# A graph-attention kernel: x loaded without zeros, first rows of Q made earlier, counting in steps, last norms side by side

## The chip, the core and the metric

The kernel runs on one core of a Trainium2 chip. A core has a matrix engine (PE; PEld is its weight load, which overlaps), a vector engine (DVE), a scalar engine (ACT), a general engine (POOL) that here issues the indirect gathers, and a queue engine (SP) that issues plain DMAs in program order. The metric is the device time of one execution in microseconds (us). All engines run their own instruction lists in order and wait for one another through semaphores.

## The reference

One layer of graph attention over 6250 nodes, 206250 edges sorted by destination, 128 features in 8 heads of 16, then a residual and a layer norm:

```python
Qh = (h @ WQ).reshape(N, H, D); Kh = (h @ WK).reshape(N, H, D); Vh = (h @ WV).reshape(N, H, D)
Eh = (edge_attr @ WE).reshape(-1, H, D)
score = jnp.einsum('ehd,ehd,ehd->eh', Kh[src], Qh[dst], Eh) * inv_sqrt_d
score = jnp.exp(jnp.clip(score, -5.0, 5.0))
msg = Vh[src] * score[:, :, None]
wV = jax.ops.segment_sum(msg, dst, num_segments=N)
Z = jax.ops.segment_sum(score, dst, num_segments=N)
h_out = wV / (Z[:, :, None] + 1e-06)
x = _layernorm(x + h_out.reshape(N, H * D), axis=-1)
```

So K and V are taken by source node (any node), Q by destination (sorted), E is a product per edge, and the sums run over edges with one destination.

## The kernel before, in words

Edges are cut into 1612 tiles of 128; four tiles make a batch, 406 batches in all (the last ones smaller). The work has a head, a loop over batches, and an end.

The head. x by features is loaded once into `xT_sb`, one column per node with a zero between every two columns (lines 113 to 116: twelve loads of an array of 2 x 6250 + 2 columns that the host has filled with zeros). The zeros belong to a trick in the loop: some tiles' columns of x are gathered on chip, two at a time, by OR-ing eight bytes (`columns`, line 371), and a zero neighbour leaves the other column as it is. The table `kv` (K and V of all nodes, in HBM) is made by `table` (line 255) in 13 groups of four blocks of 128 nodes: two engines copy from PSUM into one of two buffers `kvst`, and SP stores the buffer. Meanwhile POOL gathers rows of x for the first twelve batches (`gather`, line 392), whose K and V are then made on chip (`project`, line 412), so that they do not need the table. After the table come, in program order, `from_window(0)` (line 182), `build_q` (line 297), and the first loads `load_rel(0)` and `load_q` (lines 560 to 562).

`from_window(i)` takes the destinations of 128 (then 74) groups of eight tiles, subtracts the first node of the group, stores the result as `relD` in HBM, and counts how many edges lie within a window of 42 rows (`count`, line 175, three passes of DVE over 1024 columns). The counts prove at the end that the edges were sorted as assumed; if not, a slow path runs. `load_rel` reads `relD` back, spread over 126 partitions (`relb`). `q_rows` makes a block of 128 rows of Q as three bf16 parts, stored as `qs`; `load_q` reads the 126 rows that eight tiles need (`qw`).

The loop. For batch b, `stage_a` makes E (`eps`) and the expanded Q (`qps`) on PE; `stage_b`, one batch later, multiplies K with Q (`kq`, line 463), with E (`kqe`, 466), reduces (469) and clips (472) on DVE; `weigh` takes the exponential on ACT; `messages`, two batches later, multiplies V (`msg`, 507); `stage_c` adds up by destination on PE (`agg`, 529). Gathered rows lie in twelve buffers: POOL may gather batch b only when `msg` of batch b-12 is done. From batch 12 on gathers read `kv`. Three of every seven batches have one tile whose columns ACT and DVE copy on chip instead (lines 371 and 374). Between the stages `fill` (line 564) places one small DVE step at a time: of a block of Q, or of a layer norm.

From batch 12 on the order on each engine is the program's; before it a scheduler sets the order by readiness. SP issues its DMAs strictly one after another, and at most eight plain DMAs are in flight, as each reuses a semaphore.

The end. `finish` (line 495) shifts the sums of two blocks into place on PE, and `layernorm` (line 719) is a generator of small DVE steps. The last block is the lone one (`final`, line 522): when its last sum is made, all norms still open are run to their end first, and then its own.

Of the kernel before, what the change touches and what calls it, by code (L numbers as in the profile page):

```python
# [8 lines left out]
F32 = mybir.dt.float32  # L9
# [90 lines left out]
def edge_attention(ctx: ExitStack, tc: tile.TileContext, x, xT, srcT, srcC, dstT, dstB, dst0, bnd, lo, eaT,  # L100
# [12 lines left out]
    NX = 12  # L113
    cuts = [(2 * N + 2) * i // NX for i in range(NX + 1)]
    for a, b in zip(cuts, cuts[1:]):
        nc.sync.dma_start(spread[:, a:b], xT[:, a:b])
# [23 lines left out]
    with ExitStack() as fast:  # L140
# [34 lines left out]
        def count(rows, cl, vals, hi):  # L175

            nc.vector.tensor_scalar(cl, vals, 0.0, float(hi), op0=ALU.max, op1=ALU.min)
            nc.vector.tensor_tensor(cl, cl, vals, op=ALU.is_equal)
            nc.vector.tensor_reduce(cn[:rows, len(counts):len(counts) + 1], cl, axis=AX.X, op=ALU.add)
            counts.append(rows)  # L180

        def from_window(i):
# [7 lines left out]
            nc.vector.tensor_tensor(w[:k], d[:k, :1], bnd_c[:k, i:i + 1], op=ALU.min)  # L190
            r = ip.tile([P, WT * P], BF16, name="relq", bufs=1)
            nc.vector.tensor_scalar(r[:k], d[:k], w[:k], None, op0=ALU.subtract)
            nc.sync.dma_start(relD[a:a + k], r[:k])
            cl = wp.tile([P, WT * P], F32, name="clq", tag="kvst", bufs=2)
            count(k, cl[:k], r[:k], QW - 1)
# [25 lines left out]
        def count_inside():  # L221

            W = 4 * 2 * D
            for a in range(0, NT, W):
                e = min(NT, a + W)
                cl = wp.tile([P, W], F32, name="cl", tag="kvst", bufs=2)[:, :e - a]
                count(P, cl, rel[:, a:e], HW - 1)
# [26 lines left out]

        def table(b0):
            st = wp.tile([P, KB, 2 * D], F32, name="kvst", bufs=2)
            blocks = range(b0, min(NB, b0 + KB))
            for b in blocks:
                n = min(P, N - b * P)
                ps = pair_bank(b, "kvacc", [P, 2 * D])  # L260
                made = nc.tensor.matmul(ps[:n], xT_sb[:, b * P:b * P + n], wkv_sb,
# [3 lines left out]
                else:  # L265
                    nc.scalar.copy(st[:n, b - b0, :], ps[:n])
            full = [b for b in blocks if (b + 1) * P <= N]
# [244 lines left out]
        def stage_c(b):  # L512
            n, g, oh, m = st8.pop(b)
            for i in range(n):
# [39 lines left out]
        from_window(0)  # L554
        build_q(q_built(QLOOK + 2), True)
# [4 lines left out]
        load_rel(0)  # L560
        for j in range(QLOOK):
            load_q(j)
# [234 lines left out]
```

## Time and profile before

| | us |
|---|---|
| median of 3 runs | 1867.37 (1865.28 to 1867.83) |
| profiled execution | 1864.63 |
| its span, first to last instruction | 1862.8 |
| DVE busy | 1679.4 (90%) |
| ACT busy | 1623.1 (87%) |
| POOL busy | 1379.9 (74%) |
| PE busy | 1331.3 (71%) |
| gathers of rows of `kv` | 1401, 952 ns each |

How to read it. Times are of one execution, from the span's start. A line of the timeline has start, duration, engine, source line, operation, what is written and read, how many instructions were merged, and in brackets how long the engine was idle before and what it waited for. An engine's name with a q (SPq) is its instruction queue: issuing a DMA takes no busy time. A line of the table by stage has a stretch, its length, the busy time and number of instructions of each engine, the granted share of PE's clock, the share of time that the DMA engines were busy, and the rate they reached.

### The profile page before, as it was taken

How to read it: one execution, taken by the hardware profiler on the slowest of the kernel's cores; microseconds unless marked ns; L12 is line 12 of the kernel's file. 1: busy time of each engine (PE TensorE's matmuls, PEld its weight loads, DVE VectorE, ACT ScalarE, POOL GpSimd, SP SyncE). 2: the span in 40 equal slices, each digit the busy share in tenths (PEclk: the TensorE clock that was granted, in tenths of full speed). 3: DMA queues.
4: the chain of work that ended last, by engine and by line, in shares of the span. 5: the costliest groups of instructions: out<-in, count | busy, mean ns of one | idle time of the engine just before them, and what ended most of it. 6: DMA issues, size and time to landing. Idle time of an engine off the chain costs nothing.

```text
span 1862.8 us, 48831 instructions
## 1 busy us (share of the span) xinstructions
PE 1331.3 (71%) x9376; PEld 1163.7 (62%) x9376; DVE 1679.4 (90%) x6911; ACT 1623.1 (87%) x15506; POOL 1379.9 (74%) x1456
## 2 busy tenths in 40 slices
PE   4787777677776777676777776777767767677676
PEld 3576666666675666565666665666656656666665
DVE  3479999999999999999999999998999899998997
ACT  1236999899999999999999999999899999998993
POOL 6577777777777777777777777777777777777774
PEclk8898999899989998999999999898899899888998
DMA  9767757767777587677667667667766676667662
GB/s 316 220 196 213 219 179 209 207 201 207 207 215 208 180 241 199 184 217 228 192 209 228 190 191 225 203 185 214 219 203 186 195 231 191 195 192 227 207 195 70
DMA packets 171087, 381.63 MB, mean 205 GB/s; under 512 B 58478, under 2 KB 84412, under 8 KB 170774
## 3 DMA queue, kind: packets, MB, share of 16 engines
q0 software_dynamic: 68768, 186.80, 34.2%
q1 hardware_dynamic: 100866, 190.58, 33.7%
q14 instruction: 237, 1.94, 0.3%
q8 instruction: 76, 1.25, 0.3%
q10 hardware_dynamic: 1140, 1.06, 0.2%
HBM read 363.50 MB, written 14.81 MB: 203 GB/s over the span
## 4 chain that ended last, share of the span: by engine, by line
DVE 49%; PE 15%; DMA 12%; issue 6%; DVEq 6%; POOL 3%; ACT 0%; POOLq 0%
DMA kvrows<-kv,src 12%; DVE kqe L466 9%; DVE kq L463 9%; DVE xcol L371 8%; PE eps L453 6%; DVE sc L469 6%; DVE msg L507 5%; DVEq L364 5%; DVE onehot L431 5%; DVE onehotT L441 4%; PE agg L529 4%; POOL kvrows L401 3%; PE finps L492 3%; DVE sc L472 2%; PE qps L456 1%
## 5 line engine op out<-in xcount | busy, mean ns | idle before, releaser
L401 POOL DMA_INDIRECT kvrows<-kv,src x1401 | 1333.3, 952 | 441.9 <-issue 315.5
L374 ACT COPY xcol<-xT_sb 128x4 uint8 x14344 | 1442.7, 191 | 39.9 <-issue 33.9
L453 PE MATMUL eps<-we_sb,ea 128*128 128x128 f32 x3224 | 493.0, 300 | 446.5 <-issue 224.1
L453 PEld LDWEIGHTS eps<-we_sb,ea 128*128 128x128 f32 x3224 | 429.9, 206 | 538.6 <-issue 449.1
L529 PE MATMUL agg<-msg,onehot 128*128 128x136 f32 x3224 | 536.3, 314 | 34.0 <-DVE msg L507 23.2
L529 PEld LDWEIGHTS agg<-msg,onehot 128*128 128x128 f32 x3224 | 457.0, 212 | 86.1 <-DVE msg L507 83.5
L371 DVE TENSOR_TENSOR xcol<-xT_sb 128x8 uint8 x3260 | 301.8, 160 | 24.8 <-issue 22.2
L463 DVE TENSOR_TENSOR kq<-kvrows,qps 128x512 f32<-128x512 f32 x406 | 274.5, 676 | 51.0 <-DMA kvrows<-kv,src 26.7
L507 DVE TENSOR_TENSOR msg<-kvrows,exp_p 128x512 f32<-128x512 f32 x406 | 272.1, 670 | 4.0 <-ACT exp_p L480 4.0
L466 DVE TENSOR_TENSOR kqe<-kq,eps 128x512 f32<-128x512 f32 x406 | 272.9, 672 | 1.2 <-PE eps L453 0.8
L469 DVE TENSOR_REDUCE sc<-kqe 128x32 f32<-128x512 f32 x406 | 271.1, 668 | 0.2
L456 PE MATMUL qps<-qw,onehotT 126*128 126x128 bf16 x1612 | 169.6, 230 | 0.4 <-DVE kq L463 0.4
L431 DVE TENSOR_TENSOR onehot<-iota_p,dst_sb 128x256 f32<-128x256 f32 x406 | 167.4, 413 | 0.4 <-PE agg L529 0.4
L441 DVE TENSOR_SCALAR onehotT<-relb,node 126x512 bf16<-126x512 bf16 x406 | 148.3, 366 | 5.3 <-PE qps L456 2.7
L479 ACT ACTIVATE msg<-sc 128x32 f32<-128x32 f32 x406 | 92.9, 229 | 65.5 <-DVE sc L472 61.6
L456 PEld LDWEIGHTS <-onehotT 126*128 126x128 bf16 x1612 | 135.2, 104 | 9.4 <-issue 0.6
L383 PE MATMUL colkv<-wkv_sb,xcol 128*128 128x256 f32 x326 | 108.7, 418 | 0.0
L472 DVE TENSOR_SCALAR sc<-sc 128x32 f32<-128x32 f32 x406 | 84.5, 208 | 0.4
L492 PE MATMUL finps<-sum,shift 128*128 128x136 f32 x640 | 80.0, 282 | 0.0
L492 PEld LDWEIGHTS finps<-sum,shift 128*128 128x128 f32 x640 | 76.5, 191 | 0.0
L480 ACT ACTIVATE exp_p<-sc 128x32 f32<-128x32 f32 x406 | 74.1, 183 | 0.0
L401 POOL DMA_INDIRECT kvrows<-x,src x48 | 45.7, 952 | 21.2 <-issue 11.9
(73 smaller groups left out, 553.4 us busy)
## 6 DMA issues: line engine op xcount, KB each, us to landing
ea<-eaT SPq DMA_DIRECT2D x201, 512.0 KB
relb<-relD SPq DMA_DIRECT2D x100, 504.0 KB
kvrows<-kv,src POOLq DMA_INDIRECT x1401
qw<-qs SPq DMA_DIRECT2D x202, 31.5 KB
kv<-kvst SPq DMA_DIRECT2D x12, 512.0 KB
xT_sb<-xT SPq DMA_DIRECT2D x10, 521.0 KB
qs<-qst SPq DMA_DIRECT2D x48, 96.0 KB
xb<-x SPq DMA_DIRECT2D x24, 128.0 KB
```

The costliest lines, as they stand in the source:

```text
L371: eng.tensor_tensor(to[:, 4 * (j + c):4 * (j + c) + 8], *both, op=ALU.bitwise_or)
L374: copy(to[:, 4 * (j + c):4 * (j + c) + 4], xT_bytes[:, ds(at[c] - XT_AT, 4)])
L401: ins = nc.gpsimd.indirect_dma_start(out=g[:k, i, :f], out_offset=None, in_=rows, in_offset=bass.IndirectOffsetOnAxis(ap=src_col(t)[:k], a ...
L431: nc.vector.tensor_tensor(oh[:, :n, HW * half:HW * half + HW], iota_p[:, None, :].to_broadcast([P, n, HW]), rel[:, t0:t0 + n, None].to_bro ...
L441: nc.vector.tensor_scalar(ohT[:, :n * P], rels[t0 // RC][:, e0:e0 + n * P], node[:QROWS], None, op0=ALU.is_equal)
L453: nc.tensor.matmul(pe[:, i, :], ea[:, i * P:i * P + P], we_sb, start=True, stop=True)
L456: expanded[b] = nc.tensor.matmul(pq[:, i, :], ohT[:, i * P:i * P + P], loaded[t0 // WT], start=True, stop=True)
L463: nc.vector.tensor_tensor(t0[:, :n], g[:, :n, :D], pq[:, :n], op=ALU.mult)
L466: nc.vector.tensor_tensor(t1[:, :n], t0[:, :n], pe[:, :n], op=ALU.mult)
L469: nc.vector.tensor_reduce(sc[:, :n], t1[:, :n].rearrange("p b (h d) -> p b h d", h=H), axis=AX.X, op=ALU.add)
L507: nc.vector.tensor_tensor(m[:, :n, :D].rearrange("p b (h d) -> p b h d", h=H), g[:, :n, D:].rearrange("p b (h d) -> p b h d", h=H), exp_p[ ...
L529: nc.tensor.matmul(aggs[u][:, 0 if final else k % 2], oh[:, i, :], m[:, i, :], start=not final and t % (2 * G) == 0, stop=tail)
```

## The change

x by features is passed as a plain 128 x 6250 array. Two memsets on DVE clear the zero columns of `xT_sb`. `stage_x` loads 512 columns into a buffer of its own (four of them, shared with the tags `kq` and `kqe`); `table` takes its matmul weights from that buffer, ACT copies the buffer into `xT_sb` with the gaps, and the load for four groups later is issued before the group's store.

`from_window` and `count` become generators. The first three steps of window 0 (difference and store of `relD`), the first Q rows, `load_rel(0)` and the first `load_q` are placed after the table's second group. The other steps, and all of window 1, are taken one per batch from batch 30 on; before, window 0 was counted ahead of the loop and window 1 in batch 14.

In the last five turns of the loop only one of four `fill` places is used for norms. The last block's norm is put in front of the open ones without finishing them, and after the loop the open norms are advanced in turn, one step each.

```diff
-    NX = 12
-    cuts = [(2 * N + 2) * i // NX for i in range(NX + 1)]
-    for a, b in zip(cuts, cuts[1:]):
-        nc.sync.dma_start(spread[:, a:b], xT[:, a:b])
+    nc.vector.memset(spread.rearrange("p (n z) -> p n z", z=2)[:, :, 0], 0.0)
+    nc.vector.memset(spread[:, 2 * N + 1:], 0.0)
...
         def count(rows, cl, vals, hi):
             nc.vector.tensor_scalar(cl, vals, 0.0, float(hi), op0=ALU.max, op1=ALU.min)
+            yield
             nc.vector.tensor_tensor(cl, cl, vals, op=ALU.is_equal)
+            yield
             nc.vector.tensor_reduce(cn[:rows, len(counts):len(counts) + 1], cl, axis=AX.X, op=ALU.add)
...
             nc.vector.tensor_tensor(w[:k], d[:k, :1], bnd_c[:k, i:i + 1], op=ALU.min)
+            yield
             r = ip.tile([P, WT * P], BF16, name="relq", bufs=1)
             nc.vector.tensor_scalar(r[:k], d[:k], w[:k], None, op0=ALU.subtract)
+            yield
             nc.sync.dma_start(relD[a:a + k], r[:k])
+            yield
             cl = wp.tile([P, WT * P], F32, name="clq", tag="kvst", bufs=2)
-            count(k, cl[:k], r[:k], QW - 1)
+            yield from count(k, cl[:k], r[:k], QW - 1)
...
+        staged = {}
+        def stage_x(b0):
+            if b0 >= NB:
+                return
+            n = min(KB * P, N - b0 * P)
+            staged[b0] = wp.tile([P, KB * P], F32, name="xst", tag=("kq", "kqe")[b0 // KB % 2], bufs=2)
+            nc.sync.dma_start(staged[b0][:, :n], xT[:, b0 * P:b0 * P + n])
+
         def table(b0):
             st = wp.tile([P, KB, 2 * D], F32, name="kvst", bufs=2)
             blocks = range(b0, min(NB, b0 + KB))
+            rows, width = staged.pop(b0), min(KB * P, N - b0 * P)
+            nc.scalar.copy(xT_sb[:, b0 * P:b0 * P + width], rows[:, :width])
             for b in blocks:
...
-                made = nc.tensor.matmul(ps[:n], xT_sb[:, b * P:b * P + n], wkv_sb,
+                made = nc.tensor.matmul(ps[:n], rows[:, (b - b0) * P:(b - b0) * P + n], wkv_sb,
                                         start=True, stop=True)
...
+            stage_x(b0 + 4 * KB)
...
                 if tail and final:
-                    norms.extend(pending)
-                    pending.clear()
-                    while norms:
-                        fill()
-                    norms.append(layernorm(nc, sp, aggs.pop(u)[:, :1], xbs.pop(QL), out, QL, 1, stores))
+                    norms.insert(0, layernorm(nc, sp, aggs.pop(u)[:, :1], xbs.pop(QL), out, QL, 1, stores))
...
+        for b0 in range(0, 4 * KB, KB):
+            stage_x(b0)
+        counting = from_window(0)
         gathered = {b: gather(b) for b in range(2)}
         for b0 in range(0, NB, KB):
             made = table(b0)
+            if b0 == KB:
+                for _ in range(3):
+                    next(counting)
+                build_q(q_built(QLOOK + 2), True)
+                load_rel(0)
+                for j in range(QLOOK):
+                    load_q(j)
...
-        from_window(0)
-        build_q(q_built(QLOOK + 2), True)
+        second_half = itertools.chain(counting, from_window(1))
...
-        load_rel(0)
-        for j in range(QLOOK):
-            load_q(j)
-
...
-            elif norms and next(norms[0], None) is None:
+            elif norms and (not late or late.pop()) and next(norms[0], None) is None:
                 norms.pop(0)
...
-                if b == 14:
-                    from_window(1)
+                if b >= 30:
+                    next(second_half, None)
...
+            late[:] = [False] * 9 + [True] if b >= nbat - 2 else []
...
         while norms:
-            fill()
+            for steps in list(norms):
+                if next(steps, None) is None:
+                    norms.remove(steps)
...
-    xT = np.zeros((D, 2 * N + 2), x.dtype)
-    xT[:, 1:2 * N + 1:2] = x.T
...
-        "xT": xT,
+        "xT": np.ascontiguousarray(x.T),
```

More of the change, by code (lines that the diff above doesn't have):

```diff
@@ L1 @@
+import itertools
 from contextlib import ExitStack
@@ L226, in count_inside @@
                 cl = wp.tile([P, W], F32, name="cl", tag="kvst", bufs=2)[:, :e - a]
-                count(P, cl, rel[:, a:e], HW - 1)
+                for _ in count(P, cl, rel[:, a:e], HW - 1):
+                    pass
             nc.vector.tensor_reduce(cn[:, :1], cn, axis=AX.X, op=ALU.add)
@@ L567, in fill @@
                 build_q(0, False)
-            elif norms and next(norms[0], None) is None:
+            elif norms and (not late or late.pop()) and next(norms[0], None) is None:
                 norms.pop(0)
-        held = []
+        held, late = [], []
         for b in range(nbat + 3):
```

## The prediction

> **What bounds the kernel now.** I read the busy shares first, then busy time by stage, then the timeline around the two ends of the longest unbroken stretch, and the waits last. The page shows several engines nearly full and no winner:
>
> ```profile
> PE 1331.3 (71%) x9376; PEld 1163.7 (62%) x9376; DVE 1679.4 (90%) x6911; ACT 1623.1 (87%) x15506; POOL 1379.9 (74%) x1456
> ```
>
> The table by stage (stretch, its length, then busy us and count for PE, PEld, DVE, ACT, POOL, then clock, DMA share, GB/s) decides. The cuts are the first gather, the first gather from the table `kv`, and the end of the last gather:
>
> ```profile
> 3.67:81.70 78.03, 45.23 (x168) 34.13 (x169) 26.50 (x76) 14.72 (x36) 45.70 (x48) 0.80 0.83 281
> 81.70:1843.80 1762.10, 1278.38 (x9158) 1123.47 (x9158) 1639.03 (x6764) 1606.39 (x15458) 1333.31 (x1401) 0.93 0.69 204
> 1843.80:1862.80 19.00, 7.68 (x53) 6.08 (x52) 11.63 (x62) 1.99 (x12) 0.00 (x0) 0.82 0.07 18
> ```
>
> POOL's 74% deceives, because issuing is not counted as busy:
>
> ```profile
> 62.33 0.95 POOL L401 DMA_INDIRECT kvrows<-x,src  x1 [0.30 <-PE qrows L286]
> 63.58 0.94 POOL L401 DMA_INDIRECT kvrows<-x,src  x1 [0.30 <-issue]
> ...
> 67.57 0.94 POOL L401 DMA_INDIRECT kvrows<-x,src  x1 [0.30 <-PE xtps L416]
> 81.72 0.95 POOL L401 DMA_INDIRECT kvrows<-kv,src  x1 [13.21 <-DVE msg L507]
> ...
> 1842.86 0.90 POOL L401 DMA_INDIRECT kvrows<-kv,src  x1 [0.30 <-issue]
> ```
>
> Each gather costs 0.95 us and a fixed 0.30: one per 1.25 us (62.33 to 63.58). 1401 of them need 1751 us, and the middle stage lasts 1762. So from 81.7 to 1843.8 POOL runs without a real gap, and the time is: start of the first `kv` gather, plus 1762, plus a 19 us tail. DVE (1639 of 1762) sits just below. In the head POOL is not full: 48 gathers at 1.25 fill 60 of its 78 us. The 13.2 us gap before 81.72 ends with the first batch's `msg`, which frees the first of twelve gather buffers. So the question is when the first batch is done.
>
> **Why the first batch is late.** The head's rows in order:
>
> ```profile
> 1.22 13.54 SPq L116 DMA_DIRECT2D xT_sb<-xT  x12
> 15.62 1.73 SPq L269 DMA_DIRECT2D kv<-kvst  x2
> 27.74 0.65 ACT L266 COPY kvst<-kvacc 128x256 f32<-128x256 f32 x2 [16.16 <-DMA kv<-kvst]
> 51.41 3.80 SPq L269 DMA_DIRECT2D kv<-kvst  x2
> 59.21 0.65 ACT L266 COPY kvst<-kvacc 128x256 f32<-128x256 f32 x2 [2.65 <-DMA kv<-kvst]
> 59.64 0.69 PE L261 MATMUL kvacc<-wkv_sb,xT_sb 128*106 128x256 f32 x2 [1.30 <-ACT kvst L266]
> 62.73 0.37 ACT L266 COPY kvst<-kvacc 106x256 f32<-106x256 f32 x1 [2.87 <-DMA kv<-kvst]
> 64.39 0.69 DVE L177 TENSOR_SCALAR clq<-relq 128x1024 f32<-128x1024 bf16 x1 [2.21 <-DMA kv<-kvst]
> ...
> 65.24 1.22 DVE L178 TENSOR_TENSOR clq<-clq,relq 128x1024 f32<-128x1024 f32 x1
> 66.57 1.21 DVE L179 TENSOR_REDUCE cn<-clq 128x1 f32<-128x1024 f32 x1
> 66.71 1.11 PE L416 MATMUL xtps<-ident,kvrows 128*128 128x128 f32 x4 [4.60 <-DVE qr L291]
> 68.34 1.13 SPq L294 DMA_DIRECT2D qs<-qst  x2
> 72.32 0.59 ACT L424 COPY kvrows<-kvps 128x512 f32<-128x512 f32 x1 [1.12 <-PE kvps L423]
> 73.71 4.55 SPq L316 DMA_DIRECT2D qw<-qs  x6
> 76.78 0.69 DVE L463 TENSOR_TENSOR kq<-kvrows,qps 128x512 f32<-128x512 f32 x1 [7.68 <-PE qps L456]
> 80.78 0.68 DVE L507 TENSOR_TENSOR msg<-kvrows,exp_p 128x512 f32<-128x512 f32 x1
> ```
>
> The twelve x loads, zeros included, are 6.4 MB (2 x 6250 + 2 columns x 128 x 4 bytes). The first table store, issued at 15.62, lands only at 27.7: 12.1 us. Only two `kvst` buffers exist, so the table idles for it. The last table matmul ends at 60.3, and then 16.5 us pass until the first `kq`: rows of Q, the counting of the first window, the store and reload of Q (`qw` at 73.7).
>
> ```profile
> 8.00:12.00 4.00, 3.13 (x11) 1.82 (x10) 0.63 (x2) 2.55 (x5) 3.09 (x4) 1.00 1.02 373
> 24.00:28.00 4.00, 0.00 (x0) 0.00 (x0) 0.24 (x1) 0.26 (x1) 3.08 (x4) 0.50 1.06 391
> 32.00:36.00 4.00, 3.74 (x14) 2.85 (x13) 1.13 (x4) 0.74 (x2) 0.24 (x1) 0.83 0.63 196
> 68.00:72.00 4.00, 3.50 (x8) 2.87 (x9) 1.03 (x5) 1.03 (x2) 0.51 (x1) 0.50 0.84 239
> ```
>
> DMA is full (373 to 391 GB/s) up to about 30 us and no longer after.
>
> **Part 1, x loaded without zeros.** Bytes: 6.4 to 3.2 MB, in 13 loads of 256 KB, four ahead, the rest issued as the four buffers come free. In the new order on SP four `ea` loads (2.1 MB) and `col_at` stand ahead of the first store, so what is ahead of it on SP is 3.5 MB instead of 6.5. At 0.38 MB/us that is some 8 us less; before, the store took 12.1 us where later ones took about 4 to 6 (the second of the pair at 51.41 was issued near 54.9 and gave its buffer at 59.2; the one of 56.76 gave it at 62.7), so the queue ahead cost 6 to 8. I take the first store landing at 20.5, 7 us sooner.
>
> The page "DMA: Bandwidth & Descriptors" of the Trainium skill, section "Queues, rings and completion order", says descriptors of a ring are consumed in order on each engine; so the four early `ea` loads delay the store, which speaks against the change. The trace agrees: the 12.1 us store stood behind the x loads. By its section "Anatomy of one DMA" (2.0 us and the bytes at 436 GB/s) a 512 KB store would land in an estimated 3.2 us, and the forecast would come out an estimated 0.4 us lower (POOL's own 48 gathers, below, would then bind); the rows' 4 to 6 are used.
>
> Added on DVE: a memset of 6251 elements per partition, first in its queue.
>
> ```profile
> L154 DVE MEMSET onehot<- x8: 272/272/272, 0.9 to 2.8; 128x256 f32 x8
> ```
>
> 256 elements take 0.272, so 6251 take 6.6 us (stride 2 might double it: 13.3; nothing shows less). Behind it stand the set-up and the first `kvst` copies: 0.8 + 6.6 + about 5 us of set-up puts them at 13 to 15; DVE's second such group ran at 15.08 before, held by a small load. So it costs 0; at 13.3 the start would slip 6.
>
> Added on ACT: 13 copies of 128x512 in strided form. Nearest row: 0.59 for 128x512 (L424). 7.7 us in all; ACT has 63 idle us in this stage. 0, at most 7.7 if each stands before its group's copies. Table matmuls read contiguous rows instead of every second element: 0, PE has 33 us spare in the head.
>
> **Part 2, first Q, `relb` and `qw` behind the second table group.** Moved up: 20 small DVE and PE steps on four Q blocks, four Q stores, the window store, a 504 KB `relb` load, a register load, three `qw` loads. SP runs in order, and the `qw` loads wait for the Q stores (68.3 and 69.1 issued, 73.7 on): with Q done near 23.5 the third `qw` goes out near 30. Behind it wait the eighth x load and the fourth table store. From there two stores are in flight: (4.4 landing + 1.5 copying) / 2 = 2.95 us per group; the eight steps left put the last table matmul at 30.3 + 8 x 2.95 = 53.9 (before 60.3). Then only transpose, project and copy remain: 66.71 to 72.9 is 6.2 us at half clock, I take 5.2: first `kq` at 59, its `msg` done 4.7 later (76.78 to 81.46) at 63.7. POOL's own 48 gathers end at 3.67 + 60 = 63.6. First `kv` gather: 64.0. **-17.7 us.**
>
> **Part 3, counting in steps, window 1 from batch 30.** Before, window 1 stood whole in batch 14:
>
> ```profile
> 135.79 0.16 DVE L190 TENSOR_TENSOR wq<-dB_sb,bnd_c 74x1 f32<-74x1 int32 x1 [3.51 <-DMA dB_sb<-dstB]
> ...
> 144.28 0.94 POOL L401 DMA_INDIRECT kvrows<-kv,src  x1 [2.01 <-PE eps L453]
> ...
> 148.51 0.94 POOL L401 DMA_INDIRECT kvrows<-kv,src  x1 [0.79 <-issue]
> ```
>
> The two POOL gaps are 1.7 and 0.5 over the usual 0.30: **-2.2.** Against it: the load wait (3.5) and window 0's three passes (0.7 + 1.2 + 1.2 = 3.1 us) now fall on DVE from batch 30 on, where kq, and all batches behind it, slip. Busy time up to 200 us, of POOL's gathers and of DVE's `kq`:
>
> ```profile
> 0.00:200.00 200.00, 134.08 (x140) 0.88 0.74 236
> ...
> 0.00:200.00 200.00, 19.09 (x28) 0.88 0.74 236
> ```
>
> 140 gathers are some 36 batches (some tiles are not gathered), against 28 batches consumed: POOL is 8 of its 12 buffers ahead, so the DVE time costs POOL nothing unless the buffers fill; then up to 4. I take +0.5 for gathers stretched beside these passes.
>
> **Part 4, last norms.**
>
> ```profile
> 1845.27 0.17 DVE L727 TENSOR_SCALAR rz<-fin 128x16 f32<-128x16 f32 x1 [3.26 <-ACT fin L502]
> ...
> 1852.40 0.28 DVE L507 TENSOR_TENSOR msg<-kvrows,exp_p 128x128 f32<-128x128 f32 x1
> ...
> 1855.32 0.15 DVE L739 TENSOR_SCALAR y<-v 106x1 int32<-106x1 int32 x1
> 1855.39 0.14 DVE L741 TENSOR_SCALAR vh<-v 106x1 f32<-106x1 f32 x1
> 1855.50 0.16 DVE L743 TENSOR_TENSOR w<-y 106x1 f32<-106x1 f32 x1
> ```
>
> The 3.26 us wait stays: it precedes the thinning. Between it and the last `msg` ten small steps go, at about 0.08 each (an independent pair starts 0.07 apart): -0.8. After it, dependent steps start 0.2 apart, so the second chain fits between; two 128x128 steps do not quite: +0.3, against 0.3 saved where the last norm queued. **-0.8**; ends -2 and +1.
>
> **Sum.** -17.7 - 2.2 + 0.5 - 0.8 = -20.2. The profiled execution took 1864.6 us (span 1862.8): 1844.4. The median of the runs, 1867.37, is 2.7 above it: **1847 us**.
>
> **Rivals.** *The table stays slow (18%):* refills, stores and `qw` waits share one in-order queue. For: DMA falls to 196 GB/s at 32 us, so latency rules there. At 4.2 us per group the last matmul ends at 63.9, first `kq` at 69: -7.7 - 2.2 - 0.8, about 1857. *The gather buffers fill (9%):* POOL starts early but stalls again from batch 40, where the load wait and counting now fall. For: the gaps at 144 and 148; against: 8 of 12 at 200 us. Costs 4: 1851. *One store in flight, the slower side (10%):* if the refill standing before each store delays it until the previous one landed, a group takes 4.4 + 1.5 = 5.9; the last matmul ends at 77.5, first `kq` at 82.7, +5.9 - 2.2 - 0.8 = 1870. Against it: four loads ahead. It turns the sign at some 5.5 us per group. *Better still (5%):* POOL's idle gone and a shorter tail, 1840.
>
> **Chances.** Forecast 58%, own range 1842 to 1852. A repeat tells 0.2% from no change. Faster 0.87 (forecast, buffers, better, most of the slow table), same 0.03 (the slow table's upper end), slower 0.10. The range leaves out the best case and the slower rival: 1841 to 1860.
>
> **What would show it.** First `kv` gather on POOL near 64 instead of 81.7; first table store landing near 21; last table matmul near 54; the memset at 6.6 us; no POOL gap over 1 us after it; POOL's last gather near 1824. A group period over 5 us, POOL gaps near batch 40, or a DVE wait for `dstB` that reaches POOL would make the forecast wrong.

## The result, and the profile after

The changed kernel takes 1862.34 us (median of 11 runs, 1860.19 to 1867.17) against 1867.37 (1865.03 to 1869.42) of the kernel before beside it: a ratio of 0.9975, 95% interval 0.9966 to 0.9985. It is faster, by 5 us where the forecast had 20. The profiled execution has a span of 1860.7 us (time 1862.53), 2.1 under the span before. That is less than the 5 us between the medians, because the profiled execution of the kernel before was 2.7 us faster than its median and that of the changed kernel within 0.2 of its own. The traces below account for the 2.1.

The busy row of the changed kernel's page, engine by engine:

```profile
PE 1330.8 (72%) x9376; PEld 1158.3 (62%) x9376; DVE 1680.8 (90%) x6913; ACT 1632.9 (88%) x15519; POOL 1385.7 (74%) x1456
```

It says nothing of where the gain went; it is nearly the row of before. The table by stage of the changed kernel, cut at the same three events (first gather, first gather from `kv`, end of the last gather; columns as in the prediction), does:

```profile
3.61:68.58 64.97, 46.10 (x161) 32.76 (x162) 29.59 (x85) 21.21 (x48) 45.86 (x49) 0.79 0.89 286
68.58:1841.30 1772.72, 1277.00 (x9166) 1119.46 (x9165) 1638.61 (x6767) 1609.66 (x15459) 1338.92 (x1401) 0.93 0.68 203
1841.30:1860.70 19.40, 7.71 (x54) 6.12 (x52) 11.13 (x62) 1.99 (x12) 0.00 (x1) 0.83 0.06 17
```

The first gather from `kv` starts 13.1 us sooner (81.70 to 68.58). Then the middle stage, with the same 1401 gathers, lasts 10.6 us longer (1762.1 to 1772.7), and the tail 0.4 longer: -13.1 + 10.6 + 0.4 = -2.1, the whole difference of the spans. So the head gave most of what was promised, and the loop gave it back.

Where in the loop? Busy time and number of POOL's instructions in equal stretches, the changed kernel:

```profile
100.00:200.00 100.00, 76.18 (x79) 0.91 0.69 210
200.00:300.00 100.00, 71.81 (x74) 0.87 0.67 196
300.00:400.00 100.00, 75.14 (x79) 0.91 0.64 187
```

and the kernel before:

```profile
100.00:200.00 100.00, 74.37 (x78) 0.91 0.70 214
200.00:300.00 100.00, 75.63 (x81) 0.97 0.71 210
300.00:400.00 100.00, 75.87 (x80) 0.90 0.63 189
```

Between 200 and 300 us POOL issues 74 gathers where before it issued 81. Seven gathers at 1.25 us are 8.7 us, lost in one stretch. The timeline of the changed kernel shows that place on three engines, SP's queue, then DVE, then POOL:

```profile
195.49 0.26 SPq L188 DMA_DIRECT2D dB_sb<-dstB  x1
...
194.03 0.67 DVE L481 TENSOR_TENSOR kq<-kvrows,qps 128x512 f32<-128x512 f32 x1
210.43 0.15 DVE L191 TENSOR_TENSOR wq<-dB_sb,bnd_c 74x1 f32<-74x1 int32 x1 [11.23 <-DMA dB_sb<-dstB]
210.60 0.69 DVE L481 TENSOR_TENSOR kq<-kvrows,qps 128x512 f32<-128x512 f32 x1
...
213.00 0.68 DVE L525 TENSOR_TENSOR msg<-kvrows,exp_p 128x512 f32<-128x512 f32 x1
...
209.13 0.95 POOL L419 DMA_INDIRECT kvrows<-kv,src  x1 [0.30 <-issue]
214.41 1.44 POOL L419 DMA_INDIRECT kvrows<-kv,src  x1 [4.34 <-PE eps L471]
...
226.69 2.01 POOL L419 DMA_INDIRECT kvrows<-kv,src  x1 [0.30 <-issue]
...
249.09 1.06 POOL L419 DMA_INDIRECT kvrows<-kv,src  x1 [1.22 <-PE qps L474]
253.86 0.95 POOL L419 DMA_INDIRECT kvrows<-kv,src  x1 [1.21 <-PE qps L474]
```

SP issues the load of window 1 at 195.49; the DVE step that reads it stands in the same turn of the loop, and DVE reaches it 3.7 us later. The data come 14.9 us after the issue. DVE stands for 11.23 us, so two `kq` that should follow each other in about 5 us are 16.6 apart (194.03 to 210.60).

The gather at 214.41 is the first of batch 42. It writes the buffer that `msg` of batch 30 sets free. That `msg` starts at 213.00 and ends at 213.68, and the gather starts 0.7 us later, just as the gather at 144.28 in the kernel before starts 0.7 us after the end of `msg` of batch 12. So the twelve buffers were full. (The row names a matmul of PE that was running then. The program also ties each gather from batch 18 on to a matmul of an earlier batch, here twelve batches back; that one had been made 23 us before. In this trace it was always there at least 1.7 us before the gather that waits for it.)

How long DVE may stand before POOL feels it can be read at this gather. Without a wait POOL would have started it at 210.38 (209.13 + 0.95 + 0.30). Without its 11.23 us DVE would have ended `msg` at 202.45, and the buffer would have been ready at 203.2. So 7.2 us were free, and 11.23 - 7.2 = 4.0 is what the gap of 4.34 has over the usual 0.30. Two gaps of 1.2 follow, each ending 0.7 us after a `msg`, and some gathers run over their 0.95: the longest, 2.01 at 226.69, starts as DVE starts a counting pass (226.66).

POOL cannot win that back. It was 15.1 us ahead of the kernel before at batch 30 (156.3 against 171.4), is 15.1 ahead at batch 40, 6.6 at batch 55, 5.1 at batch 100, 3.6 at batch 205 and 2.5 at its last gather. From the 13.1 at its first `kv` gather that is +2.0 up to batch 30, -8.5 between batches 40 and 55, and another -4.1 over the 350 batches behind, for which no single place can be named.

The same load in the kernel before, in the timeline of SP:

```profile
125.69 0.27 SPq L187 DMA_DIRECT2D dB_sb<-dstB  x1
```

It was used at 135.79, 10.1 us after its issue, of which DVE waited 3.51: SP was 6.6 us ahead of DVE there, where it is 3.7 ahead in the changed kernel.

### The profile page after: what moved, and what is told of

Read it like the earlier page. It is cut to its first block, busy times and chain, and to the rows that moved or that the text cites. A ratio compares the mean times of both kernels' runs of the same rounds, so it can differ in the third digit from the quotient of the medians.

```text
span 1860.7 us, 48856 instructions
## 1 busy us (share of the span) xinstructions
PE 1330.8 (72%) x9376; PEld 1158.3 (62%) x9376; DVE 1680.8 (90%) x6913; ACT 1632.9 (88%) x15519; POOL 1385.7 (74%) x1456
## 3 DMA queue, kind: packets, MB, share of 16 engines
q8 instruction: 76, 1.25, 0.3%
## 4 chain that ended last, share of the span: by engine, by line
DVE 43%; PE 11%; DMA 11%; issue 6%; DVEq 5%; POOL 4%; ACT 2%; ACTq 0%; POOLq 0%
DMA kvrows<-kv,src 11%; DVE kqe L484 8%; DVE kq L481 8%; DVE xcol L389 7%; DVE sc L487 5%; DVE msg L525 5%; DVEq L382 5%; PE eps L471 4%; DVE onehot L449 4%; POOL kvrows L419 4%; DVE onehotT L459 3%; PE finps L510 3%; PE agg L547 2%; DVE sc L490 1%; ACT xcol L392 1%
```

## The experiments

The theory from this trace: part 3 keeps a DMA and the DVE step that reads it in one turn of the loop, at a place where DVE gets to it sooner and the load takes longer; what is lost is that wait. Rivals: the three counting passes themselves fill the buffers; the head's gain is taken back by the buffers anyway, whatever the load does; the head's moves carry less than they seem.

**A chip where POOL does not bind.** Four of the six series below ran on chips on which the kernel before takes 2535 to 2582 us. The clock granted to PE in the profiled executions there is 0.76 to 0.78, against 0.92 to 0.93 on the others, and ACT stands between its own instructions for no reason that the profile shows. ACT's waits, of the load-at-14 kernel there:

```profile
ACT xcol L395 <- issue: 547.1, 1043, 1.2
```

and of the kernel before in its own profile (the line waited for, us in total, times, longest):

```profile
ACT xcol L374 <- issue: 33.9, 127, 0.6
```

POOL is 54% busy there instead of 74%, so a gather saved or lost decides nothing, and the times of those series speak neither for nor against any theory below. What their traces show of one wait or one chain of steps still counts, and is used where it is said. The changed kernel itself was not timed on such a chip.

**1. The load of window 1 far ahead of its use.** The load is issued in batch 14; everything else is the changed kernel.

```diff
+        def load_window(i):
+            a, k = i * P, min(P, NJ - i * P)
+            dB_sb.append(ip.tile([P, WT * P], I32, name="dB_sb", bufs=1))
+            nc.sync.dma_start(dB_sb[i][:k], dstB[a:a + k])
...
-            if i == len(dB_sb):
-                dB_sb.append(ip.tile([P, WT * P], I32, name="dB_sb", bufs=1))
-                nc.sync.dma_start(dB_sb[i][:k], dstB[a:a + k])
...
+                if b == 14:
+                    load_window(1)
```

> The changed kernel, with the load of the second window's destinations issued in batch 14 and everything else (the counting steps from batch 30 on) left where it is. The changed kernel's first table gather came 13.1 us sooner (68.6 against 81.7), and 7.9 us of that went between 200 and 300 us, just after DVE had waited 11.2 us for this load. Theory T (the wait for the load gave the gain back): the wait falls under 1 us, no POOL gap over 1 us stands between 200 and 300, and the time is 1862.3 - 8 to 10 = about 1853. Rival R (the 7 us of counting steps themselves fill the twelve gather buffers): POOL still stalls near batch 43, and the time stays within 3 us of 1862.

> The same kernel as in the first run of this series (the window's load issued in batch 14), again, since on that chip the kernel before took 2535 us and DVE, ACT and POOL all waited for their own instructions, so that no wait in the loop could reach the end. Where the kernel before takes about 1867: theory T (the 11.2 us wait for the load gave the gain back) says ratio to the kernel before 0.992 (about 1853), no POOL gap over 1.5 us between 200 and 300; rival R (the counting steps fill the buffers) says 0.9975 as for the changed kernel, with a POOL gap of 4 us near 214.

> One look at the early-load kernel once more. If the kernel before takes about 1867 beside it: theory T says about 1853 and no POOL gap over 1.5 us between 200 and 300 us; rival R says about 1862 and a POOL gap of 4 us near 214. If the kernel before takes 2535 again, nothing of this can be read from the time.

> The early-load kernel with an interval. The single look gave 1850.8 beside 1866.5 for the kernel before. Theory T: ratio 0.991 to 0.993. Rival R, that the single look was lucky: 0.9975 as the changed kernel.

The first two ran on the chips where POOL does not bind: ratios 0.9986 (0.9955 to 1.0016) and 0.9998 (0.9969 to 1.0028), not to be told from no change. The third, one execution beside one of the kernel before: 1850.77 against 1866.48. The fourth: 1853.47 us (1850.34 to 1855.57) against 1864.74, ratio 0.9935, interval 0.9919 to 0.9952. That interval lies wholly below the changed kernel's 0.9966 to 0.9985; the two were not taken beside each other, but each beside the kernel before on its own chip. In the fourth's profile DVE goes straight on:

```profile
190.54 1.22 DVE L178 TENSOR_TENSOR clq<-clq,relq 128x1024 f32<-128x1024 f32 x1
191.67 0.68 DVE L484 TENSOR_TENSOR kq<-kvrows,qps 128x512 f32<-128x512 f32 x1
196.79 0.14 DVE L194 TENSOR_TENSOR wq<-dB_sb,bnd_c 74x1 f32<-74x1 int32 x1
196.86 0.67 DVE L484 TENSOR_TENSOR kq<-kvrows,qps 128x512 f32<-128x512 f32 x1
```

and POOL has no gap between 200 and 300 us:

```profile
200.00:300.00 100.00, 75.94 (x80) 0.95 0.68 209
```

The three passes of window 0 and those of window 1 are all still there, at the same batches. So the rival that the counting fills the buffers falls, and so does the one that the buffers take the head's gain back anyway. The load's wait is the cause of most of the loss. Moving one DMA is worth 0.4% here, some 7 us by the two ratios.

The passes cost something all the same. Between batches 30 and 55 POOL takes 3.0 us more than 1.25 per gather here (3.2 in experiment 2), 9.0 in the changed kernel and 0.5 in the kernel before. So of the 8.5 us lost there some 6 belong to the wait and some 2.5 to the passes, beside which gathers run long: here too one of 2.01 us, at 213.37, with a pass on DVE from 213.35. What is free at the first gather of batch 42 is not the same in every execution: 12.7 us in this one, without a wait, and 7.2 in the changed kernel's. So the gaps shown above are the price of the wait in one execution, and the ratios are the better measure.

**2. The load left in its place, in two parts.** Two loads of 64 and 10 rows instead of one of 74.

```diff
-                nc.sync.dma_start(dB_sb[i][:k], dstB[a:a + k])
+                nc.sync.dma_start(dB_sb[i][:64], dstB[a:a + 64])
+                nc.sync.dma_start(dB_sb[i][64:k], dstB[a + 64:a + k])
```

> The changed kernel, with the 74-row load of the second window split into 64 and 10 rows, at the same place. In the trace the 74-row load (296 KB) took 14.9 us from issue to the end of DVE's wait (10.1 in the kernel before), while relb of 504 KB on 126 rows took 6.1. Theory D (74 rows are spread over few DMA engines): the load lands in about 4 us, DVE's wait falls to 0 to 1 us, and the time equals that of the early load, about 1853. Rival C (the load stands in a crowd of gathers and edge loads): the wait stays at 8 to 12 us and the time near 1862. The page "DMA: Bandwidth & Descriptors" of the Trainium skill, section "Why a DMA increments its semaphore by 16 and not by 1", gives the number of engines as the largest of at most 16 that divides the rows: 2 for 74, 16 for 64 and 10 for 10; by it D holds.

> The same kernel as in the second run (the 74-row load as 64 and 10 rows, in place). There the wait fell from 10.7 to 5.3 us and issue to use from 14 to 8 us. Where the kernel before takes about 1867: theory D (few DMA engines) says the wait of DVE falls from 11.2 to between 3 and 6 and the time lies between the changed kernel's 1862 and the early load's 1853, near 1857; rival C (crowd alone) says 11 and 1862.

> The changed kernel, the 74-row load of window 1 as 64 and 10 rows, issued where the change has it. Theory D (74 rows go over few DMA engines): DVE's wait falls from 11.2 to between 0 and 6 us and the time comes to within 3 us of the early load's 1851. Rival C (the crowd of gathers and edge loads alone): the wait stays near 11 us, the time near 1862.

On the chips where POOL does not bind: 1.0004 (0.9969 to 1.0039) and 1.0004 (0.9966 to 1.0041), not to be told from no change. On the usual chip 1853.8 us, ratio 0.9945 (0.9928 to 0.9961), as good as experiment 1 within the intervals. Its timeline, SP and DVE:

```profile
192.73 0.82 SPq L188 DMA_DIRECT2D dB_sb<-dstB  x1
193.59 0.51 SPq L189 DMA_DIRECT2D dB_sb<-dstB  x1
...
201.22 0.16 DVE L192 TENSOR_TENSOR wq<-dB_sb,bnd_c 74x1 f32<-74x1 int32 x1 [5.11 <-DMA dB_sb<-dstB]
```

From the second issue to the use 7.6 us, instead of 14.9; DVE waits 5.11 instead of 11.23; and POOL has no gap over 1.5 us between 200 and 300 us. The first theory had the load landing in some 4 us and DVE not waiting; it takes twice that, and DVE waits. But the first gather of batch 42 starts 6.8 us after `msg` of batch 30 here, so that, less the 0.7, 6.1 us were free even behind the wait. So a wait of 5 us at this place costs nothing that can be measured and one of 11 some 6 to 7: what is free decides.

The 74-row load is slow mostly by its shape: on one chip where POOL does not bind it took 14.2 us from issue to use as one load (the kernel with part 4 undone, experiment 6), and 8.1 and 7.4 as two. The moment counts too: as one load it took 10.1 us in the kernel before and 12.5 in experiment 3, both in batch 14. The Trainium skill, page "DMA: Bandwidth & Descriptors", section "Why a DMA increments its semaphore by 16 and not by 1", states that a DMA is spread over the largest number of engines up to 16 that divides its rows. For 74 rows that is 2, for 64 and 10 rows it is 16 and 10. The times agree; no run here shows the number of engines.

**3. Part 3 undone.** Window 0 is counted whole ahead of the loop and window 1 in batch 14 again; parts 1, 2 and 4 stay.

```diff
-        second_half = itertools.chain(counting, from_window(1))
+        for _ in counting:
+            pass
...
-                if b >= 30:
-                    next(second_half, None)
+                if b == 14:
+                    for _ in from_window(1):
+                        pass
```

> The changed kernel with part 3 undone: window 0 is counted when its differences are there, before and between the first batches, window 1 whole in batch 14 as before. Theory T: DVE's wait for the load is again some 3 to 10 us, but 17 batches earlier, where POOL is 8 of 12 buffers ahead as well; so a stall of POOL remains and the time is 1855 to 1860. Rival R (it is the steps from batch 30 on that cost): the POOL gaps near 214 us vanish and the time is about 1852.

> The changed kernel with part 3 undone: window 0 counted between the first batches, window 1 whole in batch 14 as before. Theory T2 (a wait for this load costs as much in batch 14 as in batch 33): POOL's buffers fill near batch 26 and the time is 1855 to 1862. Rival (at batch 14 the wait is short, as the 3.5 us in the kernel before): near 1852, that is 10 us faster than the change with its counting in steps.

On the chip where POOL does not bind 0.9999 (0.9967 to 1.0032). On the usual chip 1853.28 us, ratio 0.9936 (0.992 to 0.9953): without part 3 the kernel is faster than with it, by as much as moving the load brings. The wait is there too, at 127.6, and POOL's gap behind it, at batch 24. So the gap came as the theory had it, and the time as the rival had it:

```profile
127.64 0.15 DVE L191 TENSOR_TENSOR wq<-dB_sb,bnd_c 74x1 f32<-74x1 int32 x1 [5.71 <-DMA dB_sb<-dstB]
...
136.02 0.94 POOL L419 DMA_INDIRECT kvrows<-kv,src  x1 [4.54 <-PE eps L471]
```

The load was issued at 115.11, 12.5 us before its use. So part 3 was forecast at -2.2 and +0.5 and is a loss of some 7 as it stands. With its load moved (experiment 1) it is worth nothing measurable: 1853.47 against 1853.28, on the same chip.

**4. Part 2 undone**, on top of experiment 1: Q rows, `relb` and `qw` after the whole table, as before.

```diff
-            if b0 == KB:
-                for _ in range(3):
-                    next(counting)
-                build_q(q_built(QLOOK + 2), True)
-                load_rel(0)
-                for j in range(QLOOK):
-                    load_q(j)
...
+        for _ in range(3):
+            next(counting)
+        build_q(q_built(QLOOK + 2), True)
+        load_rel(0)
+        for j in range(QLOOK):
+            load_q(j)
```

> The early-load kernel with part 2 undone: window 0's differences, the first rows of Q, relb and qw come after the table again, with x still loaded without zeros. The kernel before had 16.5 us from the last table matmul to the first kq, the changed one 5.5 (57.4 to 62.9). Theory: first kq 8 to 11 us later than in the changed kernel (near 72), the time 8 to 10 us over the early load's, about 1862. Rival (without the Q work the table ends so much sooner that it evens out): under 4 us over it.

> The early-load kernel with part 2 undone: window 0's differences, first rows of Q, relb and qw after the table. First kq near 72 instead of 62.9 and the time 8 to 10 us over the early load's, near 1860 (theory). Rival: the table ends sooner without that work, and it is less than 4 us over it.

On the chip where POOL does not bind 1.0034 (1.0000 to 1.0067). On the usual chip 1855.28 us, ratio 0.9952 (0.9935 to 0.9968), 1.8 us over experiment 1 on the same chip, and the intervals overlap. The theory's 8 to 10 us did not come, the rival's "less than 4" did. The head of this kernel, last table matmul and the gathers around the start:

```profile
49.63 0.68 PE L281 MATMUL kvacc<-wkv_sb,xst 128*106 128x256 f32 x2 [2.84 <-ACT kvst L286]
...
62.88 0.94 POOL L422 DMA_INDIRECT kvrows<-x,src  x1 [0.30 <-issue]
70.92 0.94 POOL L422 DMA_INDIRECT kvrows<-kv,src  x1 [7.10 <-DVE msg L528]
```

Without part 2 the table ends at 50.3 instead of 57.5 of the changed kernel, because no `qw` load stands in SP's queue waiting for Q. Then 15.4 us pass to the first `kq` (65.7), as 16.5 did before. With part 2 it is 5.4. Part 2 takes 10 us out of the one and puts 7 into the other. This kernel's head differs from the kernel before by part 1 and by the counting of window 0, which part 3 has taken out of the head. Its first `kv` gather is at 70.9 instead of 81.7, so these two carry 10.8 us. The table alone ends 10.0 sooner (50.3 instead of 60.3), which is part 1's; how the rest divides is not shown. Part 2 brings 0.7 to 2.7 more: with it the first `kv` gather comes at 70.2 and 69.5 (experiment 1), 68.6 (changed kernel) and 68.2 (experiment 2).

**5. Part 1 undone**, on top of experiment 1: x loaded with its zeros, no memset, no copies on ACT.

```diff
-    nc.vector.memset(spread.rearrange("p (n z) -> p n z", z=2)[:, :, 0], 0.0)
-    nc.vector.memset(spread[:, 2 * N + 1:], 0.0)
+    NX = 12
+    cuts = [(2 * N + 2) * i // NX for i in range(NX + 1)]
+    for a, b in zip(cuts, cuts[1:]):
+        nc.sync.dma_start(spread[:, a:b], xT[:, a:b])
...
-            nc.scalar.copy(xT_sb[:, b0 * P:b0 * P + width], rows[:, :width])
...
-            stage_x(b0 + 4 * KB)
```

> The early-load kernel with part 1 undone: x is loaded with its zeros by twelve loads, nothing is spread on chip. The prediction put part 1 at 7 us of the first store's landing. Theory: first table store lands near 27 again, first table gather 5 to 7 us later than with part 1 (near 75 instead of 68.6), and the time 5 to 7 us over the early load's, about 1859. Rival (POOL's own paced x gathers set the first table gather, whatever the loads do): within 2 us of the early load.

> The changed kernel with window 1's load at batch 14 and x by features loaded with its zeros, as before: 6.4 MB in twelve loads ahead of the first store, no memset, no copies on ACT. Theory (part 1 is what brings the first store and with it the table forward): first table store lands near 28 instead of 21, last table matmul near 64, first kv gather near 74, time some 5 us over load-at-14, about 1858.5. Rival (POOL's own x gathers and the Q rows set the start, part 1 is worth little): within 2 us of load-at-14, first kv gather before 72.

> As for the first kernel of this form (window 1's load at batch 14, x loaded with its zeros), on a chip where the kernel before takes some 1866 us. Theory (part 1 is what brings the table forward): first table store lands near 28, last table matmul near 64, first kv gather near 74, about 1858.5. Rival (part 1 is worth little, Q rows and POOL's x gathers set the start): first kv gather before 72, within 2 us of the 1853.5 of load-at-14.

All three came to chips where POOL does not bind: 1.0004 (0.9968 to 1.0039), 0.9992 (0.9969 to 1.0015) and 1.0007 (0.9985 to 1.0028). The first `kv` gather there is at 89.1, 90.3 and 85.1 with the zeros, and at 88.1 and 91.0 without them (experiment 1 on such a chip). So on those chips part 1 brings nothing to the head. On the usual chip part 1 undone alone was not measured; that it carries most of the gain there rests on experiment 4.

**6. Part 4 undone**, on the changed kernel and on top of experiment 1.

```diff
-                    norms.insert(0, layernorm(nc, sp, aggs.pop(u)[:, :1], xbs.pop(QL), out, QL, 1, stores))
+                    norms.extend(pending)
+                    pending.clear()
+                    while norms:
+                        fill()
+                    norms.append(layernorm(nc, sp, aggs.pop(u)[:, :1], xbs.pop(QL), out, QL, 1, stores))
...
-            late[:] = [False] * 9 + [True] if b >= nbat - 2 else []
...
-            for steps in list(norms):
-                if next(steps, None) is None:
-                    norms.remove(steps)
+            fill()
```

> The changed kernel with part 4 undone: the open norms are finished before the last one, all four places for norm steps are used to the end. Forecast of the prediction: 0.8 us slower than the changed kernel, about 1863.1. Rival (the traces after the result: from DVE's wait for the last sums to the last step 12.34 us before and 12.29 after, and 0.4 more for the stores): no difference, or 0.4 faster, 1862.

> The changed kernel with window 1's load at batch 14 and the last norms as before (the open norms are run to their end ahead of the last block's). Theory of the prediction (part 4 is worth 0.8 us): 1854.3 when load-at-14 is 1853.5, and the time from the last rz to the last step 0.8 us longer. Rival (part 4 is worth nothing, the ten small steps only move): 1853 to 1854, and rz to the last step within 0.3 us of 12.3.

Ratios 1.0025 (0.9987 to 1.0062) and 1.0019 (0.9996 to 1.0042), both on chips where POOL does not bind, not to be told from no change. But the chain of DVE steps at the end is the same there as on the usual chip, so its length can be read. From the start of the last `rz` on `fin` to the end of DVE's last step: 12.34 us in the kernel before, 12.29 in the changed one, 12.33 and 12.32 in the kernels with part 4 undone, and 12.29 in the kernels of experiments 1, 2 and 3 on such chips, which keep part 4. Up to the end of the last `msg`: 7.41 before, 7.40 undone, 7.12 changed. So part 4 brings the last `msg` 0.3 forward, the steps behind it take 0.25 longer, and 0.03 to 0.05 is left. With the small steps gone DVE waits for ACT ahead of that `msg`, on the usual chip:

```profile
1849.63 0.29 DVE L525 TENSOR_TENSOR msg<-kvrows,exp_p 128x128 f32<-128x128 f32 x1 [0.32 <-ACT exp_p L498]
```

**7. The rest of the head**, on top of experiment 1: `relb` behind the seventh table group, the three `qw` loads behind the tenth, and the x gathers no longer tied to the table's groups.

```diff
+            if b0 == 6 * KB:
                 load_rel(0)
+            if b0 == 9 * KB:
                 for j in range(QLOOK):
                     load_q(j)
...
-                gathered[b] = gather(b, made=made)
+                gathered[b] = gather(b)
```

> The changed kernel with window 1's load at batch 14, and in the table stage the reload of relb behind the 6th group, the three qw loads behind the 9th, and the x gathers no longer tied to the table's groups. Theory (the head is held by the qw loads waiting in SP's queue, and by the paced x gathers): the table ends near 51 instead of 57.5, the x gathers end near 64, the first kv gather starts at 64 to 67 instead of 68.6, and the time is some 3 us under that of load-at-14, about 1850. Rival (the two middle stages even out, since POOL's start is then set by the Q rows and the first batches anyway): within 1.5 us of load-at-14, 1852 to 1855.

> As for the first kernel of this form (the qw loads stand later in SP's queue, the x gathers are not paced), on a chip where the kernel before takes some 1866 us. Theory (these two hold the head): the table ends near 51, the first kv gather starts at 64 to 67, time about 1850. Rival (the head evens out at the Q rows and the first batches): first kv gather at 68 or later, 1852 to 1855.

Both on chips where POOL does not bind, both slower than the kernel before: 1.0051 (1.0022 to 1.008) and 1.008 (1.0048 to 1.0112). SP's queue in the first:

```profile
32.87 22.75 SPq L315 DMA_DIRECT2D qs<-qst  x2
59.49 0.34 SPq L271 DMA_DIRECT2D xst<-xT  x1
59.98 0.38 SPq L290 DMA_DIRECT2D kv<-kvst  x1
```

The x gathers do end sooner, at 64.3. But the last two Q stores are 22 us apart, with every refill and store of the table behind them; DVE makes no step in between (23.60 us of idle time before 54.64). The last table matmul ends at 94 instead of the 68.1 and 75.7 of experiment 1 on such a chip, the first `kv` gather comes at 103.8 instead of 88.1 and 91.0 (92 and 103.4 in the second run). Three things were changed at once, and which one moved the Q rows is not shown. The change failed, and what is left in the head stays untouched.

The best kernel found is that of experiment 1, at 0.9935 of the kernel before; those of experiments 2 and 3 equal it within the intervals.

## Why the prediction was right and wrong, point by point

**The step that failed** is in Part 3: "Against it: the load wait (3.5) and window 0's three passes ... the DVE time costs POOL nothing unless the buffers fill; then up to 4". The mechanism stood there, with the right batch ("stalls again from batch 40, where the load wait and counting now fall") and as a rival with 9%. Three numbers were wrong.

The wait was taken over from the row at batch 14 (3.51 us), as if it were the load's. It is the load's latency less SP's lead over DVE: 10.1 - 6.6 there, 14.9 - 3.7 = 11.2 here. The row to read would have been the load's issue in the kernel before, 10.1 us ahead of its use.

The free buffers were counted too high. "POOL is 8 of its 12 buffers ahead" counts batches by `kq`, but a buffer is set free by `msg`, which DVE makes one turn of the loop later. At 200 us of the kernel before, POOL is filling the buffer of its 37th batch and the 26th `msg` is done: 11 of 12 are in use. The `msg` of batch 24 and the first gather of batch 36, in the kernel before:

```profile
193.23 0.67 DVE L507 TENSOR_TENSOR msg<-kvrows,exp_p 128x512 f32<-128x512 f32 x1
...
197.90 0.94 POOL L401 DMA_INDIRECT kvrows<-kv,src  x1 [0.31 <-PE eps L453]
```

The gather starts 4.0 us after the `msg` that frees its buffer. Less the 0.7 of handing over, 3.3 us were free: half of the 6.6 (3.5 + 3.1) that the prediction itself put on DVE. The changed kernel had more, 7.2, but not 11.2.

And the price was capped at 4, where the middle stage lost 10.6 in all. By POOL's lead that is 2.0 gained where the two gaps went, 8.5 lost between batches 40 and 55 (some 6 by the wait and 2.5 by the passes, where the prediction had +0.5 for gathers stretched beside them), and 4.1 lost over the rest of the loop, where it had nothing. Experiments 1 and 2 show the wait's part. The cause of the 4.1 stays open; the same stretch loses 2.2 and 1.7 us in experiments 1 and 2.

**-2.2 for POOL's gaps at 144 and 148**: right. They are gone, and POOL's lead over the kernel before grew from 13.1 at its first `kv` gather to 15.1 at batch 30.

**-17.7 in the head**: measured -13.1. Its steps, on the changed kernel: ACT's copy that waited for the first store, ACT's copies of the table's end, and POOL:

```profile
20.83 0.65 ACT L283 COPY kvst<-kvacc 128x256 f32<-128x256 f32 x2 [2.17 <-DMA kv<-kvst]
...
56.42 0.65 ACT L283 COPY kvst<-kvacc 128x256 f32<-128x256 f32 x2 [4.41 <-DMA kv<-kvst]
...
36.84 0.94 POOL L419 DMA_INDIRECT kvrows<-x,src  x1 [4.33 <-PE kvacc L278]
...
67.05 0.95 POOL L419 DMA_INDIRECT kvrows<-x,src  x1 [0.31 <-PE xtps L434]
68.58 0.95 POOL L419 DMA_INDIRECT kvrows<-kv,src  x1 [0.58 <-DVE msg L525]
```

The first store landed by 20.8 (forecast 20.5). The group period was 2.95, as forecast: eight periods between the stores of 33.65 and 57.26. But the third `qw` load, and the store behind it, went out near 33 instead of 30, so the last table matmul ended at 57.5 instead of 53.9 and the first `kq` came at 62.9 instead of 59; the 5.2 us between them measured 5.4. And POOL's own 48 gathers, forecast to end at 63.6, ended at 68.0: a gather at 36.84 waited 4.33 us for a table matmul, since the x gathers are tied to the table's groups. The prediction had the 63.6 as a second floor and did not ask what that floor waits for. The kernel before has the same wait, and its x gathers end at 68.5:

```profile
37.35 0.94 POOL L401 DMA_INDIRECT kvrows<-x,src  x1 [5.11 <-PE kvacc L261]
```

In the changed kernel both chains end within a microsecond of each other at 68. In the three other executions with this head on usual chips POOL's own gathers are the later chain: they end at 69.9, 69.2 and 67.9, the first `msg` at 66.4, 68.5 and 65.4 (experiment 1 twice, experiment 2). So this floor is the step that failed in the head. In experiment 4, where POOL has no such wait, its x gathers end at 63.8, near the forecast, and the first `msg` is then what is late. The prediction's other estimate of 3.2 us for a store is worked out from a figure given for DMAs that POOL issues, while these stores go out on SP; nothing of the sum rests on it.

**The memset at 6.6 us, hidden**: right, with a reservation on the row.

```profile
2.13 5.27 DVE L114 MEMSET xT_sb<- 128x6251 f32 x1 [2.13 <-issue]
7.35 0.06 DVE L115 MEMSET xT_sb<- 128x1 f32 x1
...
13.27 0.73 DVE L281 COPY kvst<-kvacc 128x256 f32<-128x256 f32 x2
```

Its row says 5.27, but DVE, which in the kernel before starts its first step at 0.82, shows 2.13 of idle time ahead of it that ends with nothing the profile names; the next step starts at 7.35. So it costs 5.3 to 6.5 us (forecast 6.6; at the 0.272 us that 256 elements take, 6.5 from 0.82 on is the likelier), and DVE's first `kvst` copy starts at 13.27, the forecast's 13 to 15. ACT's copies of x took 0.64 to 0.68 each (forecast 0.59); that they cost nothing is not shown by itself.

**-0.8 in the tail**: wrong; 0.03 to 0.05 (experiment 6). The ten steps went from ahead of the last `msg` to behind it: it comes 0.3 sooner instead of 0.8, since DVE then waits for ACT, and what follows takes 0.25 longer. The span's tail is 0.4 longer than before. From that `rz` to the end it is 17.6 us in the kernel before, 17.9 and 18.0 in the two with part 4 undone, and 17.5 to 18.7 in those that keep it, the three at 17.5 being those with part 1 undone. So the 0.4 is not part 4's; what it is stays open.

**The rivals.** The table that stays slow was given 1857 and 18%; the table did end 3.6 later than forecast, but because the `qw` loads went out late, not by a slower period. One store in flight did not happen. The buffers that fill are the rival that came, at 9% and with 4 us where the stretch lost 8.5, some 6 of them by the wait. Against the sum of the profiled execution (1844.4 forecast, 1862.5 measured) the misses are 4.6 in the head, 12.3 in the middle stage (+10.6 where -1.7 stood) and 1.2 in the tail, 18.1 together. The range ended at 1860 because no case in it had the buffers filling and the head's refill queue late at once. The 2.7 us that the prediction put on top for the median were chance of one profiled execution, and brought its 1847 nearer to the result by luck.

## What to carry to other kernels

A DMA and the step that reads it, put into one turn of a loop on a nearly full engine, cost the DMA's latency less the queue's lead over that engine: read both from the trace of before, not the wait that happened to be left at the old place. A queue of buffers hides a stall only up to what is free: read it as the time from the end of the step that frees a buffer to the start of the step that fills it again, less the handing over, and compare it with the sum of what is put in between. Counting the buffers by another step of the same batch makes it too large. And when an early start is forecast, follow every chain that ends there, the second floor included, to what it waits for.

## What had not been expected of the hardware

- One load of 74 rows of 4 KB took 14.9 us from issue to use, and 7.6 us as 64 and 10 rows (10.1 to 14.2 and 7.4 to 8.1 in other runs).
- A gather on POOL that starts together with a counting pass of 74 x 1024 on DVE took 2.01 us instead of 0.95, in the changed kernel and in experiments 1 and 2.
- The first long memset on DVE shows 2.13 us of idle time ahead of it for which nothing is named, where a short one in its place started at 0.82; whether it is then 5.3 or 6.5 us long is not shown for certain.
- The same program takes 1865 us on one chip and 2535 on another, where ACT stands for 547 us between its own instructions (34 on the first) and the clock granted to PE is 0.76 to 0.78 (0.92 on the first); there neither an 11 us wait on DVE nor any part of the change could be told from nothing.
